# Turning all blocks with 32 by 32 transposes on VectorE and plain DMAs instead of crossbar DMA transposes

## The chip, the core and the metric

The kernel runs on one core of one Trainium2 chip. The metric is the device time of one execution in microseconds (us). A core has TensorE (PE) for matrix products, VectorE (DVE), ScalarE (ACT) and GpSimd (POOL) for elementwise work, and SyncE (SP), which here only issues DMAs. Each engine takes its instructions from a queue of its own, in order. DMAs are issued from the queues of SP and ACT.

## The reference

A layer with two residual parts on x of shape 8 x 2048 x 256 (batch, tokens, width), all in float32:

```
n1 = layernorm(x)
Q = xpos(n1 @ W_Q);  K = xpos_down(n1 @ W_K);  V = n1 @ W_V     # rotary embedding with a scale
p = softmax(Q @ K^T) * 0.9 ** |n - m|                            # softmax over all 2048 keys
x = x + p @ V
n2 = layernorm(x)
h = silu(fp4(n2) @ fp4(w_gate)^T) * (fp4(n2) @ fp4(w_up)^T)      # 704 hidden columns
x = x + fp4(h) @ fp4(w_down)^T
```

`fp4` cuts the last dimension into blocks of 16, divides each by its largest magnitude over 6, rounds to the grid 0, 0.5, 1, 1.5, 2, 3, 4, 6 with sign, and multiplies back.

## The kernel before

Tokens are worked off in 128 blocks of 128 queries, one block to a step: `step(n)` for n = 0 to 127, 16 steps to a batch. Tokens of four blocks form a group of 512; a group is normalized (`statistics`, `normalize`), turned so that the width lies on the partitions (`turn_x`), and projected to q, k (`project_rotated`, `rotate`) and v (`project_v`, `keep_v`). The first four groups are projected before the steps; later ones are prepared inside them, spread over four steps: a group is normalized and turned where n%4 is 0, v is projected where n%4 is 1, k where it is 2 and q where it is 3.

The steps are pipelined by hand: the order of the source is the order in each engine's queue (`manual_schedule`), and step n holds parts of five blocks. It computes the scores of block n against all 2048 keys in two halves (`scores`, L451), their maxima (`maximum`, L463) and exponentials (`exponentials`, L485); turns the exponentials (`turn_p`), so that keys lie on the partitions; multiplies the turned exponentials of block n-1 with the decay (`decays`, L530) and attends (`attend`, L541), where only keys within 7 blocks count, 8 to 15 blocks, because the decay makes the rest vanish; adds the residual and normalizes for the second part (`add_residual`, `normal_scales`); rounds block n-2 to fp4 (class `Fp4`: VectorE with GpSimd, L181 to L222), turns it (`turn_xq`) and multiplies with the gate and up weights (`gate_up`, L605, with the Silu L617 behind it on ScalarE); multiplies, rounds and turns the hidden values of block n-3 (`hidden`, `turn_h`); and brings block n-4 down (`down`, L646; `finish`, L652).

Each turn goes through DRAM: ScalarE splits the 32-bit values into two planes of 16-bit halves (`split`, L231), a DMA from ScalarE's queue stores the planes (`store`, L238), and a transposing DMA from SP's queue brings them back turned (`fetch`, L243). The first four groups and some of the last blocks are turned by TensorE instead, with an identity matrix.

PSUM tiles of the scores, projections, gate and up come from one pool, in turn:

```
ps_s = ctx.enter_context(tc.tile_pool(name="ps_s", bufs=3, space=bass.MemoryType.PSUM))
ps_m = ctx.enter_context(tc.tile_pool(name="ps_m", bufs=2, space=bass.MemoryType.PSUM))
```

A tile waits until the tile that had its buffer before has been read. The weights of the second part are rounded to fp4 and turned once; their stages (`scale_weights`, `round_weights`, `turn_ffn_weights`) are spread over the projection of the first groups and steps 0 to 3 by the table `IN_STEPS`.

Of the kernel before, what the change touches and what calls it, by code (L numbers as in the profile page):

```python
# [9 lines left out]
F32 = mybir.dt.float32  # L10
I32 = mybir.dt.int32
U16 = mybir.dt.uint16
# [10 lines left out]
BAND = 7  # L23
QBLK = 16
# [9 lines left out]
def preln_xpos_retention_fp4_ffn_kernel(  # L34
# [108 lines left out]
    load_tables()  # L143
    load_pair("q", w_q)
    load_tables()
    wv_sb = cpool.tile([P, HC, H], F32, name="wv_sb")
    nc.sync.dma_start(wv_sb, w_v.rearrange("(c p) d -> p c d", p=P))
# [4 lines left out]
    wd_t = cpool.tile([P, FC, H], F32, name="wd_t")  # L152

# [74 lines left out]
    def split(planes, at, src):  # L228

        n = src.shape[-1]  # L230
        nc.scalar.copy(  # L231
            planes[:, :, at : at + n], src.bitcast(U16).rearrange("p (k h) -> p h k", h=2)
        )

    def store(planes, name):
        rows, _, n = planes.shape
        there = dram.tile([rows, 2, n], U16, tag=f"turn{rows}_{n}", name=f"there_{name}")
        nc.scalar.dma_start(there, planes)  # L238
        return there

    def fetch(dst, there):

        nc.sync.dma_start_transpose(dst.bitcast(U16), there.rearrange("q h k -> (q h) k"))  # L243
# [5 lines left out]

    def split_hidden(planes, src):  # L250
        split(planes, 0, src[:, : (FC - 1) * P])
        split(planes, (FC - 1) * P, src[:, F - P :])
# [9 lines left out]
    def load_ffn_weights():  # L262
        for name, src in (("g", w_gate), ("u", w_up)):
            raw = act_p.tile([P, FULL - 1, H], F32, tag="kt", bufs=2 * NG, name=f"w{name}_rows")
            nc.sync.dma_start(
                raw, src[: (FULL - 1) * P, :].rearrange("(c p) k -> p c k", p=P)
            )
            weight_rows[name] = raw
        whole = act_p.tile([P, 2 * GROUP], F32, tag="kt", bufs=2 * NG, name="wgu_rows")
        raw = whole[:, : 3 * H].rearrange("p (c k) -> p c k", c=3)  # L270
        for c, src in enumerate((w_gate, w_up)):
            nc.sync.dma_start(raw[:, c, :], src[(FULL - 1) * P : FULL * P, :])
            nc.sync.dma_start(raw[c * REST : (c + 1) * REST, 2, :], src[FULL * P :, :])
        weight_rows["r"] = raw
        scratch["r"] = whole[:, 3 * H :]
        big = act_p.tile([P, 2 * GROUP], F32, tag="kt", bufs=2 * NG, name="wbig")
        down_rows = []
        for c in range(HC):
            down_rows.append(act_p.tile([P, BPG * H], F32, tag="vt", bufs=6, name=f"wd_rows{c}"))
            weight_rows["d", c] = down_rows[c][:, :F]  # L280
            scratch["gu"[c]] = down_rows[c][:, F:]
        for key in "gur":
            raw = weight_rows[key].rearrange("p c k -> p (c k)")
            weight_fp4[key] = Fp4(raw, P, raw.shape[-1], f"w{key}", big, scratch[key])
        for c in range(HC):
            weight_fp4["d", c] = Fp4(weight_rows["d", c], P, F, f"wd{c}")

    def load_decay_and_down():
        nc.sync.dma_start(decay_sb, decay)
        for c in range(HC):  # L290
            nc.sync.dma_start(weight_rows["d", c], w_down[ts(c, P), :])

    def turn_ffn_weights(key):
        raw = weight_rows.pop(key)
        planes = prob_p.tile([P, 2, 2 * GROUP], U16, tag="planes", bufs=3, name=f"pl_w{key[0]}")
        if key[0] == "d":
            planes = planes[:, :, : FC * P]
            split(planes, 0, raw[:, : (FC - 1) * P])
            nc.vector.memset(planes[:, :, (FC - 1) * P : (FC - 1) * P + LAST].bitcast(F32), 0.0)
            split(planes, (FC - 1) * P + LAST, raw[:, (FC - 1) * P :])  # L300
            fetch(wd_t[:, :, ts(key[1], P)], store(planes, f"wd{key[1]}"))
        elif key == "r":
            planes = planes[:, :, : 3 * H]
            split(planes, 0, raw.rearrange("p c k -> p (c k)"))
            there = store(planes, "wr")
            for c, dst in enumerate((wg_t, wu_t)):
                fetch(dst[:, :, (FULL - 1) * P : FULL * P], there[:, :, c * H : (c + 1) * H])
                fetch(dst[:, :, FULL * P :], there[c * REST : (c + 1) * REST, :, 2 * H :])
        else:
            n = FULL - 1  # L310
            for kc in range(HC):
                nc.scalar.copy(
                    planes[:, :, kc * n * P : (kc + 1) * n * P].rearrange("p h (c k) -> p h c k", c=n),
                    raw.bitcast(U16)[:, :, kc * 2 * P : (kc + 1) * 2 * P].rearrange(
                        "p c (k h) -> p h c k", h=2
                    ),
                )
            there = store(planes, f"w{key}")
            dst = {"g": wg_t, "u": wu_t}[key]
            for kc in range(HC):  # L320
                fetch(
                    dst[:, kc, : n * P].rearrange("p (c r) -> p c r", c=n),
                    there[:, :, kc * n * P : (kc + 1) * n * P],
                )
# [6 lines left out]
    def round_weights(key):  # L331
# [4 lines left out]
        (0, "exponentials"): [(round_weights, "u")],  # L336
        (0, "end"): [(round_weights, "r"), (turn_ffn_weights, "u")],
        (1, "decays"): [(scale_weights, ("d", 1))],
        (1, "end"): [(turn_ffn_weights, "r")],
        (2, "decays"): [(round_weights, ("d", 0))],  # L340
        (3, "exponentials"): [(turn_ffn_weights, ("d", 0))],
        (3, "decays"): [(round_weights, ("d", 1))],
        (3, "end"): [(turn_ffn_weights, ("d", 1))],
    }

    def weights_in_step(n, place):
        for stage, key in IN_STEPS.get((n, place), ()):
            stage(key)
# [20 lines left out]

    def turn_x(k):  # L370
        xt = groups.pop(k)
        xn_t = act_p.tile([P, BPG, HC, P], F32, tag="xn_t", bufs=3, name=f"xnt_{k}")
        if k < NG:
            pt = ps_s.tile([P, BPG, HC, P], F32, tag="s", name=f"pt_x_{k}")
# [3 lines left out]
            for c in range(0, BPG, 2):  # L378
                nc.scalar.copy(xn_t[:, c : c + 2], pt[:, c : c + 2])
        else:  # L380
            planes = prob_p.tile([P, 2, 2 * GROUP], U16, tag="planes", bufs=3, name=f"pl_x{k}")
            split(planes, 0, xt.rearrange("p c d -> p (c d)"))
            fetch(xn_t.rearrange("p c h t -> p (c h) t"), store(planes, f"x{k}"))
# [21 lines left out]
    def rotate(k, name):  # L405
# [12 lines left out]
        load_tables()  # L418
# [21 lines left out]
    total = B * NB  # L440

# [34 lines left out]
    stored, turned = {}, {}  # L476

    def exponentials(n):

        nmax = raw_scores.pop(n)  # L480
        sums = small.tile([P, 2], F32, tag="sums", name=f"sums_{n}")
        prs = []
        for half in range(2):
# [8 lines left out]
            prs.append(pr)  # L492
        stored[n] = []
        for half in range(2):
            keys = keys_of(n, half)
            if keys and n == total - 1:
                stored[n] = (keys, prs[half][:, (keys[0] - half * HALF) * P :])
            elif keys:
                w, at = len(keys) * P, (keys[0] - half * HALF) * P
                planes = prob_p.tile([P, 2, HALF * P], U16, tag="planes", bufs=3, name=f"pl_{n}_{half}")  # L500
                split(planes, 0, prs[half][:, at : at + w])
                stored[n].append((keys, store(planes[:, :, :w], f"p{n}_{half}")))
        prob[n] = sums

    def turn_p(n):
        p_t = prob_p.tile([P, 2 * BAND + 1, P], F32, tag="p_t", name=f"p_t_{n}")
        if n == total - 1:
            keys, pr = stored.pop(n)
            pt = ps_s.tile([P, HALF, P], F32, tag="s", name=f"pt_p_{n}")
            for j in range(len(keys)):  # L510
                nc.tensor.transpose(pt[:, j, :], pr[:, ts(j, P)], ident)
            turned[n] = (p_t, pt)
            return
        first = stored[n][0][0][0]
        for keys, there in stored.pop(n):
            fetch(p_t[:, keys[0] - first : keys[-1] + 1 - first, :], there)
        turned[n] = (p_t, p_t)
# [7 lines left out]
    def decays(n):  # L525
        keys, (p_t, pt) = band(n), turned[n]
        for c in range(0, len(keys), BPG):
            w = min(BPG, len(keys) - c)
            d0 = keys[c] - n % NB + BAND
            nc.vector.tensor_tensor(  # L530
                p_t[:, c : c + w, :], pt[:, c : c + w, :], decay_sb[:, d0 : d0 + w, :], ALU.mult
            )

    attended = {}

    def attend(n):
        b, i = divmod(n, NB)
        po = ps_m.tile([P, H], F32, tag="m", name=f"o_{n}")
        keys, (p_t, _) = band(n), turned.pop(n)
# [10 lines left out]
    def inverse_sum(n):  # L550
        sums = prob[n]
        rs = small.tile([P, 1], F32, tag="rs", name=f"rs_{n}")
        nc.vector.tensor_tensor(rs, sums[:, 0:1], sums[:, 1:2], ALU.add)
        nc.vector.reciprocal(rs, rs)
        prob[n] = rs
# [3 lines left out]
    def add_residual(n):  # L559
        x1 = ffn_p.tile([P, H], F32, tag="x1", bufs=5, name=f"x1_{n}")  # L560
# [21 lines left out]
    def turn_xq(n):  # L582
        x1, xq, _ = mid.pop(n)
        xq_t = ffn_p.tile([P, HC, P], F32, tag="xq_t", bufs=1, name=f"xq_t_{n}")
        if n >= total - 2:
# [3 lines left out]
            nc.scalar.copy(xq_t, pt)  # L589
        else:  # L590
            planes = ffn_p.tile([P, 2, FC * P], U16, tag="hplanes", name=f"pl_xq{n}")[:, :, :H]
            split(planes, 0, xq)
            fetch(xq_t, store(planes, f"xq{n}"))
# [263 lines left out]
```

## Time and profile before

| | |
|---|---|
| median of 3 runs | 2896.73 us (2894.92 to 2897.74) |
| the profiled execution | 2900.07 us, its span 2898.2 us |
| busy PE, DVE, ACT, POOL | 2826.7, 2280.1, 1431.8, 1410.7 us |
| mean granted TensorE clock | 0.990 |
| DMA | 446.24 MB in 892828 packets, 730992 of them under 512 B |
| SP's queue (q1), ACT's queue (q10) | 43.0% and 18.4% of 16 engines' span |

The profile is of one execution. A row of its groups gives line, engine, operation, what is written from what, the count, then busy time and mean duration, then the idle time of the engine just before and what ended it. A line of the waits names who waited for whom, in total, how often, and the longest. A timeline row gives start, duration, engine and instruction. A row of the DMA issues gives the size of each and the median time from issue to landing. PE's busy time is modelled from pipelined matrix products, so a few us of it are uncertain.

### The profile page before, as it was taken

The page shows a single profiled execution, that of the slowest core. Times are in us where ns is not written, and L with a number is a line of the kernel's source. Part 1 is how long each engine was busy: PE and PEld are TensorE (multiplying, and loading weights), DVE is VectorE, ACT ScalarE, POOL GpSimd, SP SyncE. Part 2 cuts the span into 40 slices and gives each one's busy share as a digit, 9 for nine tenths or more (in the row PEclk, how much of TensorE's full clock was granted, in tenths as well). Part 3 has the DMA queues.
Part 4 walks back from the last instruction along what each step waited for, and adds up shares of the span by engine and source line. Part 5 has one row for each costly group of instructions (what it writes and reads, how often), then busy time and mean ns, then how long its engine had stood idle before and what let it go on. Part 6 is the DMA issues. An engine that isn't in the chain of part 4 may idle for free.

```text
span 2898.2 us, 31875 instructions
## 1 busy us (share of the span) xinstructions
PE 2826.7 (98%) x9668; PEld 1839.3 (63%) x9668; DVE 2280.1 (79%) x5249; ACT 1431.8 (49%) x1592; POOL 1410.7 (49%) x1328
## 2 busy tenths in 40 slices
PE   7789999999999999999999999999999999999997
PEld 4456666666666666666666666666666666666665
DVE  7677788777888777877877878877788877777787
ACT  2345455554555554555554555554454554455552
POOL 5455454544554445544455454454445454444443
PEclk9899999999999999999999999999999999999998
DMA  5567565775567665577565666566656666546651
GB/s 177 143 152 176 147 162 140 179 177 142 144 166 160 169 165 142 152 180 172 147 159 145 162 170 161 144 175 160 167 144 157 160 171 145 141 125 147 159 133 43
DMA packets 892828, 446.24 MB, mean 154 GB/s; under 512 B 730992, under 2 KB 839920, under 8 KB 892656
## 3 DMA queue, kind: packets, MB, share of 16 engines
q1 hardware_dynamic: 786640, 266.04, 43.0%
q10 hardware_dynamic: 106016, 178.16, 18.4%
q8 instruction: 77, 1.26, 0.2%
q14 instruction: 95, 0.78, 0.1%
HBM read 71.04 MB, written 194.90 MB: 92 GB/s over the span
## 4 chain that ended last, share of the span: by engine, by line
PE 81%; DVE 9%; POOL 4%; issue 2%; DMA 2%; ACT 1%; ACTq 0%; SPq 0%; POOLq 0%; DVEq 0%
PE s L451 26%; PE o L541 18%; PE d L646 10%; PE gate L605 9%; PE up L605 9%; PE pp_k L394 3%; PE pp_q L394 3%; PE pv L425 3%; DVE m L463 1%; DVE p_t L530 1%; POOL h L221 1%; POOL h L220 1%; DMA xq_t<-there_xq 1%; POOL h L222 1%; DVE h L215 1%
## 5 line engine op out<-in xcount | busy, mean ns | idle before, releaser
L451 PE MATMUL s<-kt,qt 128*128 128x512 f32 x2048 | 909.0, 596 | 13.7 <-ACT h L617 7.8
L451 PEld LDWEIGHTS s<-kt,qt 128*128 128x128 f32 x2048 | 389.4, 191 | 478.0 <-issue 419.6
L541 PE MATMUL o<-v,p_t 128*128 128x256 f32 x2944 | 658.6, 380 | 8.2 <-DVE p_t L530 8.2
L541 PEld LDWEIGHTS o<-v,p_t 128*128 128x128 f32 x2944 | 560.4, 191 | 87.4 <-DVE p_t L530 9.9
L220 POOL TENSOR_TENSOR h<-h,big_h 128x704 f32<-128x704 f32 x126 | 212.1, 1684 | 553.2 <-DVE big_h L219 549.1
L463 DVE TENSOR_REDUCE m<-s 128x1 f32<-128x1024 f32 x256 | 310.3, 1213 | 97.8 <-PE s L451 97.2
L231 ACT COPY pl<-p 128x2048 uint16<-128x2048 uint16 (+7 forms) x239 | 357.6, 1496 | 58.1 <-ACT pl L231 49.5
L646 PE MATMUL d<-wd_t,h_t 128*128 128x256 f32 x1536 | 360.8, 385 | 14.5 <-issue 4.4
L231 ACT COPY pl_xq<-xq 128x512 uint16<-128x512 uint16 x126 | 77.8, 618 | 600.7 <-POOL xq L222 600.7
L646 PEld LDWEIGHTS d<-wd_t,h_t 128*128 128x128 f32 x1536 | 294.8, 193 | 102.2 <-issue 38.6
L485 ACT ACT_TABLE_LOAD x125 | 160.4, 1283 | 352.1 <-DVE nmax L468 301.3
L605 PE MATMUL gate<-wg_t,xq_t 128*128 128x352 f32 x1024 | 324.4, 460 | 4.4 <-DMA xq_t<-there_xq 3.9
L605 PE MATMUL up<-wu_t,xq_t 128*128 128x352 f32 x1024 | 323.8, 459 | 0.0
L231 ACT COPY pl_h<-h 128x1280 uint16<-128x1280 uint16 x248 | 194.0, 829 | 250.3 <-POOL h L222 248.3
L485 ACT ACTIVATE p<-s,nmax 128x1024 f32<-128x1024 f32 x256 | 282.8, 1110 | 20.0 <-DVE nmax L468 17.8
L195 POOL TENSOR_TENSOR h<-h,inv_h 128x704 f32<-128x704 f32 x126 | 174.5, 1385 | 225.8 <-DVE inv_h L193 225.8
L605 PEld LDWEIGHTS up<-wu_t,xq_t 128*128 128x128 f32 x1024 | 194.6, 190 | 108.3
L605 PEld LDWEIGHTS gate<-wg_t,xq_t 128*128 128x128 f32 x1024 | 194.0, 190 | 94.3 <-ACT pl L231 4.2
L530 DVE TENSOR_TENSOR p_t<-p_t,decay_sb 128x512 f32<-128x512 f32 (+3 forms) x414 | 243.7, 645 | 1.3 <-DMA p_t<-there_p 1.3
L195 POOL TENSOR_TENSOR xq<-xq,inv_x 128x256 f32<-128x256 f32 x127 | 78.8, 620 | 302.1 <-DVE inv_x L193 299.7
L221 POOL TENSOR_TENSOR h<-h,big_h 128x704 f32<-128x704 f32 x126 | 211.6, 1679 | 9.9
L220 POOL TENSOR_TENSOR xq<-xq,big_x 128x256 f32<-128x256 f32 x127 | 92.3, 726 | 238.7 <-DVE big_x L219 238.7
(139 smaller groups left out, 3475.9 us busy)
## 6 DMA issues: line engine op xcount, KB each, us to landing
there_p<-pl ACTq DMA_DIRECT2D x127, 512.0 KB, 3.2
there_h<-pl_h ACTq DMA_DIRECT2D x124, 384.0 KB, 4.1
rope_k<-in_rope_dram SPq DMA_DIRECT2D x32, 512.0 KB, 4.5
rope_q<-in_rope_dram SPq DMA_DIRECT2D x32, 512.0 KB, 4.9
xr<-in_L_attn_X_dram SPq DMA_DIRECT2D x128, 128.0 KB, 3.2
out_dram<-x SPq DMA_DIRECT2D x128, 128.0 KB, 3.5
there_xq<-pl_xq ACTq DMA_DIRECT2D x126, 128.0 KB, 2.1
x<-in_L_attn_X_dram SPq DMA_DIRECT2D x31, 512.0 KB, 4.8
```

The source lines that it names most:

```text
L195: self.wide_on.tensor_tensor(self.v3, self.v3, self.wide(inv), ALU.mult)
L220: self.wide_on.tensor_tensor(v, v, big, ALU.add)
L221: self.wide_on.tensor_tensor(v, v, big, ALU.subtract)
L231: nc.scalar.copy(planes[:, :, at : at + n], src.bitcast(U16).rearrange("p (k h) -> p h k", h=2))
L394: nc.tensor.matmul(pp[:, half, :], w_pair[name][:, hc, half, :], xn_t[:, :, hc, :], start=(hc == 0), stop=(hc == HC - 1),)
L451: nc.tensor.matmul(ps[:, j, :], q[:, dc, ts(i % BPG, P)], kt[b, half * 2 + j][:, dc, :], start=(dc == 0), stop=(dc == 1),)
L463: nc.vector.tensor_reduce(raw_scores[n][:, half : half + 1], raw_scores[n, half], AX.XY, ALU.max)
L485: nc.scalar.activation(pr, raw_scores.pop((n, half)).rearrange("p j k -> p (j k)"), AF.Exp, bias=nmax, accum_out=sums[:, half : half + 1],)
L530: nc.vector.tensor_tensor(p_t[:, c : c + w, :], pt[:, c : c + w, :], decay_sb[:, d0 : d0 + w, :], ALU.mult)
L541: nc.tensor.matmul(po, p_t[:, j, :], vt[b, k // BPG][:, k % BPG, :], start=(j == 0), stop=(j == len(keys) - 1),)
L605: nc.tensor.matmul(ps[:, half, :FH], xq_t[:, hc, :], w[:, hc, ts(half, FH)], start=(hc == 0), stop=(hc == HC - 1),)
L646: nc.tensor.matmul(pd, h_t[:, fc, :], wd_t[:, fc, :], start=(fc == 0), stop=(fc == FC - 1))
```

## The change

Nine things change; the arithmetic of the result stays what it was.

1. Turns of p, xq, h and x inside the steps no longer use 16-bit planes and transposing DMAs. The new `turn` transposes every 32 by 32 square on VectorE into a tile `sq`, with the squares' columns grouped by quarter; one DMA from ScalarE's queue stores it; four plain DMAs from SP's queue, one for each 32 partitions, bring back rows whose runs are a quarter of the width: 64 elements for xq, 192 for h, 256 for x, 256 to 480 for p. What arrives still has its runs in the order quarter, square, element (`in_runs`).
2. ScalarE copies xq, h and x out of that order (`keep_xq`, `keep_h`, `keep_x`); for p the product with the decay reads through it. `p_t` and the new `runs` have one buffer. `sq` of p and of x is one tile with one buffer; xq and h have their own.
3. Groups after the first are normalized by ScalarE (`normalize_on_scalar`: a negated mean, four passes that add it, four that scale), not by VectorE.
4. The two halves' sums are added by ScalarE behind the exponentials; VectorE keeps the reciprocal.
5. The weights are turned by TensorE with ScalarE copies; their loads, scales, rounds and turns stand at other places.
6. In a step `turn_h` stands after the residual, `turn_x` after `turn_h` and before `normal_scales`; `turn_xq` after the scales of h; step 2 attends before it projects.
7. Tables of the rotation (`load_tables`) are loaded after the attention of a step, not inside `rotate`.
8. Blocks 120 to 123 (`deferred`) keep their turned hidden values in tiles of the keys' pool, and their `down` and `finish` move behind the last step.
9. The memset of `wd_t`'s unused rows moves to the start.

```diff
+    def turn(dst, pieces, name, tag):
+        n = sum(src.shape[-1] for src in pieces) // NSQ
+        sq = prob_p.tile([P, dst.shape[-1]], F32, tag=tag, bufs=1, name=f"sq_{name}")
+        sq = sq[:, : NSQ * n].rearrange("p (c f) -> p c f", c=NSQ)
+        at = 0
+        for src in pieces:
+            w = src.shape[-1] // NSQ
+            nc.vector.transpose(
+                sq[:, :, at : at + w].rearrange("p c (k i) -> p k c i", i=SQ),
+                src.rearrange("p (k c i) -> p k c i", c=NSQ, i=SQ),
+            )
+            at += w
+        there = dram.tile([NSQ, SQ, NSQ, n], F32, tag=f"turn_{n}", name=f"there_{name}")
+        nc.scalar.dma_start(there.rearrange("a i c f -> (a i) c f"), sq)
+        dst = dst[:, : NSQ * n].rearrange("p (a f) -> p a f", a=NSQ)
+        for c in range(NSQ):
+            nc.sync.dma_start(dst[ts(c, SQ)], there[:, :, c, :].rearrange("a i f -> i a f"))
...
+    def normalize_on_scalar(k, blocks=range(BPG)):
+        xt, (mv, rstd) = groups[k], normed.pop((k, blocks))
+        minus = small.tile([P, BPG], F32, tag="minus", bufs=2, name=f"minus_{k}")
+        nc.scalar.mul(minus, mv[:, :, 0], -1.0)
+        for c in blocks:
+            nc.scalar.activation(xt[:, c, :], xt[:, c, :], AF.Identity, bias=minus[:, c : c + 1])
+        for c in blocks:
+            nc.scalar.mul(xt[:, c, :], xt[:, c, :], rstd[:, c : c + 1])
...
-            planes = prob_p.tile([P, 2, 2 * GROUP], U16, tag="planes", bufs=3, name=f"pl_x{k}")
-            split(planes, 0, xt.rearrange("p c d -> p (c d)"))
-            fetch(xn_t.rearrange("p c h t -> p (c h) t"), store(planes, f"x{k}"))
+            xt = groups[k].rearrange("p c d -> p (c d)")
+            turn(xt, [xt], f"x{k}", "sq")
...
+        rs = small.tile([P, 1], F32, tag="rs", name=f"rs_{n}")
+        nc.scalar.activation(rs, sums[:, 0:1], AF.Identity, bias=sums[:, 1:2])
...
+            runs = prob_p.tile([P, (2 * BAND + 1) * P], F32, tag="runs", bufs=1, name=f"runs_{n}")
+            turn(runs, pieces, f"p{n}", "sq")
...
-            planes = ffn_p.tile([P, 2, FC * P], U16, tag="hplanes", name=f"pl_xq{n}")[:, :, :H]
-            split(planes, 0, xq)
-            fetch(xq_t, store(planes, f"xq{n}"))
+            turn(xq, [xq], f"xq{n}", "sq_x")
...
+            turn(h, [h[:, : (FC - 1) * P], h[:, F - P : F]], f"h{n}", "sq_h")
...
     IN_STEPS = {
-        (0, "exponentials"): [(round_weights, "u")],
-        (0, "end"): [(round_weights, "r"), (turn_ffn_weights, "u")],
-        (1, "decays"): [(scale_weights, ("d", 1))],
-        (1, "end"): [(turn_ffn_weights, "r")],
+        (0, "maximum"): [(scale_weights, ("d", 0))],
+        (0, "exponentials"): [(scale_weights, ("d", 1))],
+        (0, "rotation"): [(round_weights, "u")],
+        (0, "attend"): [(turn_ffn_weights, "g")],
+        (1, "decays"): [(round_weights, "r")],
+        (1, "attend"): [(turn_ffn_weights, "u")],
         (2, "decays"): [(round_weights, ("d", 0))],
-        (3, "exponentials"): [(turn_ffn_weights, ("d", 0))],
+        (2, "attend"): [(turn_ffn_weights, "r")],
         (3, "decays"): [(round_weights, ("d", 1))],
+        (3, "attend"): [(turn_ffn_weights, ("d", 0))],
         (3, "end"): [(turn_ffn_weights, ("d", 1))],
     }
...
         scores(n, 1)
+        if on(3):
+            hid[n - 3][2].normalize()
         if on(2):
             turn_xq(n - 2)
-        if on(3):
-            hid[n - 3][2].normalize()
         maximum(n, 1)
+        if on(4) and n - 4 < total - 4:
+            keep_h(n - 4)
         exponentials(n)
+        if on(2) and n - 2 < total - 2:
+            keep_xq(n - 2)
+        for g in kept:
+            keep_x(g)
...
-            normalize(k)
+            normalize_on_scalar(k)
...
-        if on(3) and n < total - 1:
-            turn_h(n - 3)
...
         if on(1):
             add_residual(n - 1)
+        if on(3) and n < total - 1:
+            turn_h(n - 3)
+        if turn_group:
+            turn_x(k)
+            kept.append(k)
+        if on(1):
             normal_scales(n - 1)
         if on(2):
             gate_up(n - 2)
-        if turn:
-            turn_x(k)
         weights_in_step(n, "end")
```

## The prediction

> **What bounds the kernel now.** I read the page's busy line, then busy time by stage, the waits, the timeline of one step, and last the rows that price the new work.
>
> ```profile
> PE 2826.7 (98%) x9668; PEld 1839.3 (63%) x9668; DVE 2280.1 (79%) x5249; ACT 1431.8 (49%) x1592; POOL 1410.7 (49%) x1328
> ```
> ```profile
> 0.00:160.00 160.00, 122.56 (x336) 66.99 (x337) 111.61 (x243) 47.63 (x59) 83.92 (x69) 0.89 0.57 157
> 160.00:2780.00 2620.00, 2601.72 (x8967) 1702.45 (x8966) 2077.67 (x4810) 1342.84 (x1483) 1283.94 (x1219) 1.00 0.63 157
> 2780.00:2898.00 118.00, 102.43 (x368) 69.83 (x366) 90.84 (x197) 41.32 (x51) 42.85 (x40) 0.93 0.30 74
> ```
> Columns of a stage: length, then busy PE, PEld, DVE, ACT, POOL, then clock. In 2620 us of steady steps PE stands still for 18 us. The head loses 37 us and runs at a clock of 0.89, the tail loses 16 us. The steady part has little to give and much to lose.
>
> ```profile
> DVE xq L573 <- POOL rstd_f L159: 155.8, 127, 3.6
> DVE x L561 <- PE o L541: 134.4, 75, 2.9
> PE s L451 <- ACT h L617: 7.8, 7, 3.0
> ```
> VectorE's idle time lies in waits of its own queue, which new work may fill. The third line is the tightest place of the loop: `ps_s` has three PSUM buffers, so the second half of a step's scores takes the buffer that the Silu of the step before has read. The timeline of a step n with n%4=0 and the start of n+1 shows it:
>
> ```profile
> 1479.38 7.03 PE L451 MATMUL s<-kt,qt 128*128 128x512 f32 x16
> 1485.30 0.43 DVE L193 RECIPROCAL inv_h<-scale_h 128x44 f32<-128x44 f32 x1
> 1486.44 1.23 DVE L463 TENSOR_REDUCE m<-s 128x1 f32<-128x1024 f32 x1 [0.72 <-PE s L451]
> 1491.33 0.20 ACT L485 ACTIVATION_READ_ACCUMULATOR p<-s,nmax 128x1 f32 x1
> 1494.17 1.68 POOL L221 TENSOR_TENSOR h<-h,big_h 128x704 f32<-128x704 f32 x1
> 1494.41 0.48 DVE L561 SCALAR_TENSOR_TENSOR x<-o,rs,xr 128x256 f32<-128x256 f32 x1
> 1497.02 3.60 PE L451 MATMUL s<-kt,qt 128*128 128x512 f32 x8
> 1498.95 0.34 ACTq L238 DMA_DIRECT2D there_h<-pl_h  x1
> 1500.61 0.76 ACT L617 ACTIVATE h<-gate 128x704 f32<-128x704 f32 x1
> ```
> From 1479.38 on: exponentials end at 12.15; the scores of n+1 start at 17.64, and their second half is due 3.43 later, at 21.07. The Silu ends at 21.99, which is 2.42 after the store of h was issued (table load and Silu lie between), and PE lost 0.8 us there. This was a step with 8 blocks of attention; each further block gives PE 0.43 us more.
>
> **The change, part by part.**
>
> ```profile
> L181 DVE TENSOR_REDUCE amax_h<-h 128x44 f32<-128x704 f32 x128 | 112.5, 879 | 0.1
> L181 DVE TENSOR_REDUCE amax_x<-xq 128x16 f32<-128x256 f32 x128 | 53.7, 420 | 4.4
> L553 DVE TENSOR_TENSOR rs<-sums 128x1 f32<-128x1 f32 x128 | 153.2, 1197 | 0.0
> L366 DVE TENSOR_SCALAR x<-x,mv,rstd_a 128x256 f32<-128x256 f32 x128 | 44.1, 407 | 4.9 <-POOL rstd_a L159 4.9
> L138 ACT COPY wk_pair<-wk_raw 128x256 f32<-128x256 f32 x2 | 0.7, 416 | 4.0 <-DMA wk_raw<-in_L_attn_W_K_dram 4.0
> ```
> ```profile
> there_p<-pl ACTq DMA_DIRECT2D x127, 512.0 KB, 3.2
> there_xq<-pl_xq ACTq DMA_DIRECT2D x126, 128.0 KB, 2.1
> x<-in_L_attn_X_dram SPq DMA_DIRECT2D x4, 128.0 KB, 2.4
> ```
> *VectorE.* No row is a 32x32 transpose. The two reductions give 156 ns + 1.025 ns per element[...]. L219 (538 ns for 704, 294 for 256) would be the floor, 155 + 0.545 per element; twice the reduction the ceiling. I take the reductions, as a transpose also reads one f32 stream: p (11.5 blocks, 1472 elements, 1.9 instructions) 1.81 us, xq 0.42, h (640+128) 1.10, x (1024) 1.21. Over 127, 126, 124 and 28 uses: 230 + 53 + 136 + 34 = 453 us. L553 goes: it is a one-column addition of two SBUF operands, and its 1197 ns last until the GpSimd instruction beside it ends, so 153 us go and nothing is put behind it but a reciprocal (164 ns). Would a transpose be held in the same way? L561 above, with one SBUF tensor, takes its usual 0.48 us in the middle of L221; a transpose has one, so I say no. L366 goes for 31 groups (1.38 us each): -43. Sum 2280 + 453 - 153 - 43 = 2537 us, 87%; floor 2370, ceiling 2990. Most of it falls into the waits above: the transposes of h stand where VectorE waited for rstd_f, those of p where L553 stood, those of xq in the 0.72 us before L463.
>
> *ScalarE.* All splits go (358 + 78 + 194 us by their groups); copies of h (0.8 us), xq (0.4), x (1.0), a one-column sum (about 0.25) and the normalization come. Less work, but in one queue, in order. The Trainium skill says that additions and multiplications belong on VectorE, not ScalarE ("ScalarE: Activation LUTs", Rules for kernel authors), which speaks against this part. Rows: four L366 take 1.38 us; ScalarE needs eight passes at 0.37 to 0.45 (L138) plus the negated mean, about 4.3 us with the waits on its own results. By load alone the rule costs nothing (ScalarE is at 49%); by place it decides, as follows.
>
> *Where it lands.* In a step with n%4=0 ScalarE's order is: exponentials, sum, copy of xq, eight normalizing passes, then the store of p, store of h, store of x, Silu. The copy of xq waits for the new round trip: transposed at 6.3 to 6.75 (in VectorE's gap), store issued 6.85, 2.2 us to SP's start as now, four loads at 0.5 each, the last landing 2.2 after its issue: 12.8, copied by 13.2. Passes to 17.4. The store of p, issued there, lands at 20.6. And the tile `sq`, one buffer, serves p and x: the transposes of x (`turn_x`) wait for that landing. They end at 21.75, the store of x is issued at 21.85, the Silu ends 2.42 later at 24.3, instead of 21.07 due. PE waits 3.2 us, now 0.8. For 11, 15 and 12 blocks PE is due at 22.4, 24.1, 22.8; p's store has 768, 960, 704 KB, at the page's 0.0027 us per KB more (512 against 64 KB, 3.2 against 2.0) the Silu ends at 25.0, 25.5, 24.8: waits 2.6, 1.4, 2.0. Four such steps cost 2.4 + 2.6 + 1.4 + 2.0 = 8.4 us more than now; 27 steps turn a group in the loop after n=1: **+56 us**. Bounds: were p to land by 17.4, nothing; with each term at its slow end (passes 0.5, loads 3 us) 1.5 us more per step, +96.
>
> Queued on VectorE behind the stalled transposes, by their durations in the same timeline: normal scales to 24.2, L623 (it needs the Silu, 24.3) 25.2, rounding xq 26.2, largest h 27.1, first maximum 28.2, scales of h 30.3, xq turned 30.7, second maximum 32.1, first decay product 32.8. PE, itself late, ends the scores at 27.9 and after v (3.46) and `down` (2.59) wants the product at 34.0: no second stall. In the steps with n%4=1, along statistics, `turn_p`, residual, `turn_h`, the Silu ends within 0.2 us of PE's need, so up to 1 us each (+27) goes in the range. `gate` waits 0.4 us for xq in 7 steps: +3.
>
> *DMA.* A turn is now one store and four plain loads of 32 partitions: SP issues some 15 DMAs a step for 7 before, 8 us of 22.6 at 0.5 each; `load_tables`, moved behind p's loads, still has most of a step before its rotation, and `runs` and `p_t` with one buffer are overwritten only after the product and the attention of the step before, over 10 us earlier: nothing for these; if SP were late by a step, the rotation would wait some 4.5 us. The skill warns that a plain DMA that transposes by strides is 19 times slower than the crossbar one ("VectorE: DVE Perf Modes", The three transpose paths). By that rule xq's 2.7 us would become 51 and every step stop. But it speaks of large innermost strides; here the elements are already turned and runs are 256 to 1920 bytes. The row near it is the x load, 1 KB runs, 2.4 us. I use the row, and leave the rule a rival.
>
> *Weights.* 34 transposes on PE at 0.11 us (L377, eight in 0.87): +4. Their scale and round stages are moved on DVE and POOL, the loads behind x and tables on SP, `wd_t`'s memset to POOL's start. The head's waits before (6.8 us at L394, 7.4 at L541, 3.6 and 2.4 for POOL's rotation of kt) change: without L366 of groups 2 and 3, VectorE reaches the second rotation 7 us sooner, and the first scores end near 53 instead of 62.7; but at n=1 eight passes, p's store and the weights' copy stand before `keep_v`, for which the scores of step 2 wait some 10 us. I take -10, range -25 to +10.
>
> *Tail.* Four `down` (2.59 us each) leave the last four steps, which then are VectorE's (some 17.7 for 19.5): -7; at the end they fill PE's gaps, keep its clock up (L646 5.5 for 2.75 now), and add four L652 (0.41): -1.
>
> **Sum:** 56 + 3 + 4 - 10 - 8 = +45 on the profiled execution's 2900.1 us, 2945; that execution is 3.3 above the median, so 2942.
>
> **The rivals.** *(A) The shared `sq` buffer*, above: 2942, chance 0.57. For it: the order in ScalarE's queue and the 0.8 us that PE loses there already. *(B) All is hidden, faster:* if p's store lands by about 17.4 (passes overlapping, loads quick), the Silu ends before 21 to 24, PE runs through and even the 8 us of waits for it now go: 4 - 10 - 8 - 8 = -22, 2875. It decides where p's landing comes 3 us earlier than I have it. 0.17. *(C) VectorE becomes the bound:* transposes at half rate, 3.6 us more a step, 23.4 busy for PE's 22.0, and up to 1 us a step that it can't fill: 2995 to 3120; held by GpSimd like L553, only p's: about 2975. 0.18. *(D) Plain loads slow* at 256 bytes: xq 2.5 us later, n%4=0 and 1 wait for it, 64 x 1 to 2.5 on top of A: 3000 to 3100. 0.08.
>
> **How the numbers follow.** A's own range is 2905 to 2985. 0.2% (6 us) is what a measurement here tells from no change. Faster: B, but for 0.02, and 0.01 of A: 0.16; same: 0.02 of B, 0.04 of A: 0.06; slower the rest, 0.78. The range 2878 to 3025 leaves out the better half of B (0.08) and the upper parts of C and D (0.12).
>
> **What would show it.** Right: PE's scores waiting for Silu some 1.5 to 3 us at n%4=1, about 27 times; the x transposes waiting for p's store; PE's busy time near 2820; DVE at 85 to 88%; a transposed 1024 at 1.2 us; ScalarE busy near 1150. Wrong: no such wait (B), a transpose over 2 us for 1024 elements or held while GpSimd runs (C), `gate` waiting for the copy of xq in most steps (D).

## The result, and the profile after

The changed kernel takes 2936.84 us (median of 4 runs, 2931.39 to 2941.99) against 2897.23 us of the kernel before in the same session: a ratio of 1.0138, 95% interval 1.0118 to 1.0157, slower by 39.6 us. Its profiled execution took 2931.39 us, span 2929.6; before, 2900.07 and 2898.2. The two profiles thus differ by 31.4 us, and these are what can be located. The profiled execution of the changed kernel is its fastest, with a mean granted clock of 0.994; the other three have 0.991 or 0.992 and take 5 to 11 us more (see the last section).

First the busy line and the stages of the changed kernel, with the same columns as before (length; busy PE, PEld, DVE, ACT, POOL; clock, DMA share, GB/s):

```profile
PE 2827.4 (97%) x9702; PEld 1840.6 (63%) x9702; DVE 2469.3 (84%) x5636; ACT 1075.9 (37%) x1637; POOL 1412.5 (48%) x1329
```
```profile
0.00:160.00 160.00, 130.89 (x403) 76.17 (x404) 118.08 (x257) 52.77 (x103) 88.34 (x75) 0.94 0.44 139
160.00:2780.00 2620.00, 2565.70 (x8831) 1676.58 (x8830) 2233.24 (x5109) 980.27 (x1475) 1267.83 (x1201) 1.00 0.52 155
2780.00:2929.00 149.00, 130.85 (x472) 87.89 (x470) 118.02 (x272) 42.82 (x60) 56.37 (x54) 0.98 0.29 92
```

PE's work is as long as before, 2827 us. In the same 2620 us of the middle PE now stands still for 54 us, not 18. The waits (total, times, longest) name what it stands for:

```profile
PE d L677 <- ACT h_t L668: 57.9, 41, 3.0
...
PE o L561 <- DVE p_t L546: 16.5, 6, 5.6
...
PE s L473 <- ACT h L641: 3.8, 2, 3.4
...
DVE sq_x L237 <- DMA there_p<-sq_p: 3.2, 5, 1.4
```

The first line is new and larger than the whole loss: `down` (L677) waits for `h_t`, the copy of the turned hidden values. The last two are those that the prediction built on. The scores' wait for the Silu shrank (7.8 before, 3.8 now), and the x transposes wait 3.2 us for p's store in the whole kernel.

Where it lies is seen from PE's first score matmul in each step. For steps 16 to 111, six batches, the mean length by place in the batch is:

| n mod 16 | 0 | 4 | 8 | 12 | 1 | 5 | 9 | 13 | the other eight |
|---|---|---|---|---|---|---|---|---|---|
| before, us | 17.65 | 18.94 | 20.67 | 19.37 | 23.05 | 23.07 | 24.18 | 22.61 | |
| after, us | 19.00 | 20.83 | 23.38 | 21.22 | 21.10 | 22.82 | 24.12 | 22.39 | equal within 0.01 |

The steps with n%4=0, where no projection stands between the scores and `down`, lose 7.80 us a batch; those with n%4=1 win 2.48; six times the difference is the +32.0 of this stretch. The steps 112 to 126, which have no projections, lose 10.4: from 114 to 123 PE stands at least 1.06 us in each. The head wins: step 0 starts 2.9 us earlier, steps 0 to 15 are 5.9 shorter in all (step 7 starts 14.4 earlier, then steps 8 and 12 lose 5.6). The last step's start to the end is 2.2 shorter. Sum: 32.0 + 10.4 - 2.9 - 5.9 - 2.2 = +31.4.

Two timelines of the changed kernel show the wait (start, duration, engine, instruction, in brackets the idle time before and its releaser). The first is a step that begins at 1485.49:

```profile
1482.24 1.04 DVE L237 STREAM_TRANSPOSE sq_h<-h 128x640 f32<-128x640 f32 x2
...
1483.31 0.33 ACTq L243 DMA_DIRECT2D there_h<-sq_h  x1
...
1485.49 7.03 PE L473 MATMUL s<-kt,qt 128*128 128x512 f32 x16
...
1486.72 1.74 SPq L246 DMA_DIRECT2D h<-there_h  x4
...
1491.79 0.39 DVE L237 STREAM_TRANSPOSE sq_xq<-xq 128x256 f32<-128x256 f32 x1
...
1492.21 0.33 ACTq L243 DMA_DIRECT2D there_xq<-sq_xq  x1
...
1492.73 0.83 ACT L668 COPY h_t<-h 128x768 f32<-128x768 f32 x1 [7.01 <-DVE sq_xq L237]
...
1493.62 2.86 PE L677 MATMUL d<-wd_t,h_t 128*128 128x256 f32 x12 [1.09 <-ACT h_t L668]
```

The scores end at 1492.52 and `down` is next on PE, but on ScalarE the copy L668 stands behind the issue of xq's store, which waits for VectorE's transposes of xq. In another such step, begun at 1304.26, it is the landing of h itself:

```profile
1303.96 0.43 SPq L106 DMA_DIRECT2D rope_q<-in_rope_dram  x1
...
1304.44 0.57 SPq L684 DMA_DIRECT2D out_dram<-x  x1
...
1306.42 2.43 SPq L246 DMA_DIRECT2D h<-there_h  x4
...
1313.14 0.83 ACT L668 COPY h_t<-h 128x768 f32<-128x768 f32 x1 [8.61 <-DMA h<-there_h]
...
1314.03 2.86 PE L677 MATMUL d<-wd_t,h_t 128*128 128x256 f32 x12 [2.74 <-ACT h_t L668]
```

SP issued the rotation table of the next group (512 KB) and the output ahead of h's loads. That happens where n%4 is 2 and 3, and a block turned where n%4=3 is brought down where n%4=0.

### The profile page after: what moved, and what is told of

Read it like the earlier page. It is cut to its first block, busy times and chain, and to the rows that moved or that the text cites. A ratio compares the mean times of both kernels' runs of the same rounds, so it can differ in the third digit from the quotient of the medians.

```text
span 2929.6 us, 34597 instructions
## 1 busy us (share of the span) xinstructions
PE 2827.4 (97%) x9702; PEld 1840.6 (63%) x9702; DVE 2469.3 (84%) x5636; ACT 1075.9 (37%) x1637; POOL 1412.5 (48%) x1329
## 3 DMA queue, kind: packets, MB, share of 16 engines
q8 instruction: 76, 1.25, 0.2%
## 5 line engine op out<-in xcount | busy, mean ns | idle before, releaser
L561 PE MATMUL o<-v,p_t 128*128 128x256 f32 x2944 | 663.7, 382 | 16.5 <-DVE p_t L546 16.5
L668 ACT COPY h_t<-h 128x768 f32<-128x768 f32 x120 | 99.8, 832 | 855.7 <-DMA h<-there_h 422.1
L677 PE MATMUL d<-wd_t,h_t 128*128 128x256 f32 x1488 | 348.6, 384 | 57.9 <-ACT h_t L668 57.9
L677 PEld LDWEIGHTS d<-wd_t,h_t 128*128 128x128 f32 x1488 | 280.9, 191 | 150.6 <-ACT h_t L668 91.7
L546 DVE TENSOR_TENSOR p_t<-runs,decay_sb 128x512 f32<-128x512 f32 (+3 forms) x414 | 235.0, 625 | 7.2 <-DMA runs<-there_p 3.7
L237 DVE STREAM_TRANSPOSE sq_p<-p 128x1024 f32<-128x1024 f32 (+7 forms) x239 | 223.3, 969 | 0.0
L581 DVE SCALAR_TENSOR_TENSOR x<-o,rs,xr 128x256 f32<-128x256 f32 x124 | 60.0, 483 | 154.0 <-PE o L561 150.6
```

What stands on the lines that cost most here:

```text
L237: nc.vector.transpose(sq[:, :, at : at + w].rearrange("p c (k i) -> p k c i", i=SQ), src.rearrange("p (k c i) -> p k c i", c=NSQ, i=SQ),)
L546: nc.vector.tensor_tensor(p_t[:, c:to, :].rearrange("p k (a i) -> p k a i", a=NSQ), pt[:, c:to], decay_sb[:, d0 + c : d0 + to, :].rearrang ...
L561: nc.tensor.matmul(po, p_t[:, j, :], vt[b, k // BPG][:, k % BPG, :], start=(j == 0), stop=(j == len(keys) - 1),)
L677: nc.tensor.matmul(pd, h_t[:, fc, :], wd_t[:, fc, :], start=(fc == 0), stop=(fc == FC - 1))
```

## The experiments

Each kernel is the changed one with the edit shown, or with the edits named; times are medians, ratios are to the kernel before in the same session and have their 95% interval. The kernel before took 2897.2 to 2901.1 us in these sessions, so a difference of medians from two sessions can be some 4 us off; where it matters I give what the ratios make of it too. Theory H: h's new round trip, with its copy, ends after `down` is due. Theory A: the prediction's shared buffer. Theory V: VectorE's added work.

**A buffer of its own for x.**
```
-            turn(xt, [xt], f"x{k}", "sq")
+            turn(xt, [xt], f"x{k}", "sq_g")
```


> The x turns get a buffer of their own, so that turn_x no longer waits for the landing of p's store. Theory A of the prediction (the shared buffer holds the Silu and with it the next scores, +56 us): 2937 falls by about 56 to some 2881. Theory H (h's new round trip ends after `down` is due; 53 us of PE's waits before L677 in the steps with n%4=0 and in the last 16): the trace of the changed kernel has only 0.2 to 0.3 us of wait at the x transposes, so 0 to -3 us, 2934 to 2937. Theory C (VectorE's load is the bound): no change.

Measured: 2944.80 us, ratio 1.0159 (1.0137 to 1.0181); the changed kernel has 1.0138. Nothing of the 56 us comes back, though the wait of the x transposes for p's store, 3.2 us in the changed kernel, is gone from the trace. Theory A falls for this kernel.

**The copy of h ahead of xq's store.**
```
+        if on(4) and n - 4 < total - 4:
+            keep_h(n - 4)
         if on(2):
             turn_xq(n - 2)
         maximum(n, 1)
-        if on(4) and n - 4 < total - 4:
-            keep_h(n - 4)
```


> keep_h stands before turn_xq, so on ScalarE the copy of h is no longer queued behind the store of xq, which waits for VectorE's transposes of xq. Theory H: 21 of PE's waits before L677 (22 us) had a copy that was released by the transposes of xq; these go, the 17 whose copy was released by the landing of h (32 us) stay: -15 to -22, 2915 to 2922. Theory A and theory C: no change, or up to +5 as xq lands later.

Measured: 2939.98, ratio 1.0149 (1.0131 to 1.0166): no gain, a miss for H as I had it. In the trace no copy is released by xq's transposes any more, but 32 of the 34 waits before `down` now follow a late landing of h, and PE waits nearly as long (53.9 us). The steps with n%16=0 and 12 became shorter by 0.8 and 0.25 us, those with 4 and 8 longer by 1.3 and 1.1. In these two the landing of h came last already, so there was nothing to win; and with the copy first, xq's store waits for h's landing (in n%16=8 it leaves 9.0 us into the step, not 6.7).

**The turn of h ahead of the residual.**
```
+        if on(3) and n < total - 1:
+            turn_h(n - 3)
         if on(1):
             add_residual(n - 1)
-        if on(3) and n < total - 1:
-            turn_h(n - 3)
```


> turn_h stands before add_residual again, as in the kernel before, so h's store leaves about 1.3 us earlier. Theory H: only the 17 waits that ended with the landing of h shrink, and not below the 1.06 us that the queue behind xq sets: 32 - 17 x 1.06 = 14 us at most, so -8 to -14, 2923 to 2929. Theory A: the Silu's chain is not moved by this, no change. Theory C: no change.

Measured: 2958.55, ratio 1.0210 (1.0196 to 1.0224): slower. One line of its waits shows what the edit did to VectorE (13.4 us in 14 places in the changed kernel):

```profile
DVE sq_h L237 <- POOL h L221: 166.1, 99, 3.8
```

VectorE now stands in front of the transposes of h until GpSimd has rounded h, and the residual stands behind them. PE's wait for h_t grew to 65.8 us, not less, and that for decay products from 16.5 to 20.0.

**`down` behind the attention on PE.**
```
-        if on(4) and n - 4 not in deferred:
-            down(n - 4)
         ...
         if on(1) and n != 2:
             attend(n - 1)
+        if on(4) and n - 4 not in deferred:
+            down(n - 4)
```


> On PE `down` of block n-4 follows the attention of block n-1 instead of standing before it: it is due about 3.5 to 6.5 us later, nothing else is moved. Theory H: the whole wait before L677 goes (53 us), and at most some 5 to 10 us of waits of the attention for the decay products come: -40 to -53, 2884 to 2897. Theory A and theory C: no change (2937).

Measured: 2995.67, ratio 1.0336 (1.0322 to 1.0350): far slower, and no test of H. I moved `down` on PE but left `finish` where it was on VectorE, ahead of the residual:

```profile
DVE x L683 <- PE d L677: 262.8, 103, 5.5
...
PE o L561 <- DVE p_t L546: 101.2, 44, 5.4
```

PE's wait for h_t is gone but for 1.9 us; VectorE blocks on `down` instead, and the attention, due earlier on PE, waits for decay products.

**The table loads behind h's loads.**
```
-        for name, g in parts(n):
-            if name != "v":
-                load_tables()
         if on(4) and n - 4 not in deferred:
             finish(n - 4)
         ...
             turn_h(n - 3)
+        for name, g in parts(n):
+            if name != "v":
+                load_tables()
```


> The load of the next rotation table (512 KB, in the steps with n%4 = 2 and 3) is issued by SP behind h's four loads instead of ahead of them and of the output. Theory Q (h's loads are late because in SP's queue, and on the DMA engines, the 512 KB table goes ahead of them in the very steps before n%4=0): the 17 waits before L677 that ended with the landing of h shrink to the 1.06 us that the copy behind xq's store sets, -10 to -20, 2917 to 2927. Theory S (h's trip is simply too long in its serial parts: transposes behind the residual, store 3.6, four issues 1.7, landing 2 to 3, copy 0.8): no change, within 5 us of 2937.

Measured: 2916.18, ratio 1.0052 (1.0039 to 1.0064): 20.7 us of the 39.6 come back by the medians, 25 by the ratios, 15.5 between the two profiled executions. The five executions now agree within 1.4 us, at a mean clock of 0.995. The longest wait of `down` falls from 3.0 to 1.5 us:

```profile
PE d L677 <- ACT h_t L668: 45.1, 41, 1.5
```

What the table had delayed is the transfer, not the issue: over the steps with n%4=3 from 19 to 107, the first of h's loads follows its store by 4.05 us in the changed kernel and 4.01 here, but the latest copy of h begins 7.61 us into the next step instead of 9.13.

**Both: table loads late and the copy of h first.** The edit is the sum of the second and the fifth.

> The same, and the copy of h stands before the transposes of xq as in e2_keep_h_first. Theory Q: both causes of the wait before L677 are gone in the steps with n%4=0, -30 to -45, 2892 to 2907. Theory S: as e2_keep_h_first, 2935 to 2942.

Measured: 2899.33, ratio 0.9995 (0.9986 to 1.0003): 37.5 us come back (41 by the ratios), and the kernel is level with the one before. Both edits are needed: the copy alone brought nothing, together with the table it brings 17 us beyond the table.

```profile
PE d L677 <- ACT h_t L668: 26.1, 27, 2.1
```

**The copy in two halves,** on top of that:
```
-        nc.scalar.copy(
-            h_t.rearrange("p c (a i) -> p c a i", a=NSQ), in_runs(h) if src is None else src
-        )
+        to = h_t.rearrange("p c (a i) -> p c a i", a=NSQ)
+        src = in_runs(h) if src is None else src
+        for c in range(0, FC, FC // 2):
+            nc.scalar.copy(to[:, c : c + FC // 2], src[:, c : c + FC // 2])
```


> As e6_tables_keep, and the copy of h into h_t is two copies of three chunks each, so that `down` can begin about 0.4 us earlier. Theory H (what is left of the wait before L677, 26 us in 27 places, is the end of h's serial trip): 0.4 us less in each, -8 to -15 against e6_tables_keep, 2884 to 2892. Theory V (VectorE's queue sets those steps, and PE would wait for the decay products instead): no change, 2896 to 2903.

Measured: 2887.41, ratio 0.9962 (0.9949 to 0.9976), 11.9 us less (10 by the ratios). 0.4 us on the end of h's trip is worth that much over 27 waits; VectorE, whose work is the same, does not set these steps.

```profile
PE d L678 <- ACT h_t L671: 14.3, 18, 1.6
```

**Only h back to planes and the crossbar.**
```
-            turn(h, [h[:, : (FC - 1) * P], h[:, F - P : F]], f"h{n}", "sq_h")
         ...
+            planes = ffn_p.tile([P, 2, FC * P], U16, tag="hplanes", bufs=1, name=f"pl_h{n}")
+            split(planes, 0, h[:, : (FC - 1) * P])
+            split(planes, (FC - 1) * P, h[:, F - P : F])
+            fetch(h_t, store(planes, f"h{n}"))
         ...
-        if on(4) and n - 4 < total - 4:
-            keep_h(n - 4)
```
`split`, `store` and `fetch` come back from the kernel before.

> Only h goes back to ScalarE's split into planes and one transposing DMA straight into h_t; p, xq and x stay with VectorE's transposes, all else as in the changed kernel. Theory H (h's trip with its copy is what the change loses by): the wait before L677 (53 us) goes, and with it the slower matmuls behind each wait; steps with n%4=0 return to about 17.7, 19.0, 20.7 and 19.4 us as before, the steps with n%4=1 keep what they won: -50 to -70, 2867 to 2887, faster than the kernel before. Theory V (VectorE's 189 us more, and not h, is what the change loses by): VectorE is relieved of h's 136 us of transposes in the middle of each step, so -10 to -30 at most and waits of the attention for the decay products stay: 2907 to 2927.

Measured: 2897.82, ratio 0.9987 (0.9978 to 0.9995): 39 us come back (44 by the ratios), less than H's 50 to 70 and more than V's 30. With the table still ahead, `down` keeps a part of its wait:

```profile
PE d L702 <- DMA h_t<-there_h: 14.6, 17, 2.4
```

**The same with the table loads late.** The edit is the sum of this one and the fifth.

> As e7_h_planes (h by planes and a transposing DMA, the rest new), and the table loads behind h's load in SP's queue. Theory Q: the 17 waits of `down` for the landing of h that e7_h_planes still had (14.6 us, and the slower matmuls behind them) shrink, -10 to -20, 2878 to 2888. Theory V: the wait passes to the attention, which waits for decay products: 2893 to 2900.

Measured: 2881.84, ratio 0.9945 (0.9933 to 0.9958). The cost of the table ahead of h is now shown twice: 21 us by the medians and 25 by the ratios with the new way of turning h, 16 and 12 with the old. The steps 16 to 111 take 2094.9 us, 6.5 fewer than in the kernel before.

**The group normalized by VectorE again.**
```
-            normalize_on_scalar(k)
+            normalize(k)
```


> A group is normalized by VectorE's four L366 again (1.4 us a group) instead of ScalarE's eight passes and the negated mean (4.3 us); nothing else. By the prediction's theory A the passes hold p's store and through it the Silu: -56, about 2881. By the Trainium skill's rule (additions and multiplications on VectorE) a gain as well. Theory H: the passes are off the path; VectorE's 1.4 us come before p's transposes, which wait for the exponentials there: 2932 to 2942, no change.

Measured: 2958.27, ratio 1.0192 (1.0179 to 1.0206): slower than the changed kernel by 0.0054 of the ratio (16 us; 21 by the medians), where one theory expected a large gain and the other none. PE's wait for h_t hardly grew (57.9 before the edit), while its busy time rose from 2827.4 to 2846.4 us:

```profile
PE d L677 <- ACT h_t L668: 61.2, 46, 3.0
```

Of these 19 us, 10 lie in the steps with n%4=0 of 16 to 111, where PE ran at a lower clock behind a wait in seven steps, in the profiled execution of the changed kernel in one (last section). Besides, the head is 6.5 us longer than in the changed kernel and the steps with n%16=1 lose 1.0 us each.

**Without the deferral of four `down`,** on top of planes and late tables:
```
-    deferred = {n: None for n in range(total - 8, total - 4)}
+    deferred = {}
     ...
-    first, second, third, fourth = deferred
-    down(first)
     ...
```
The other `down` and `finish` of the deferred blocks behind the last step go too.

> As e10_planes_tables, without the deferral of four `down` to the end. The prediction's step (-7 in the last four steps, -1 at the end): 8 us slower than e10_planes_tables. What the trace of the changed kernel suggests (in steps 124 to 126 PE stands 2.2 to 3.0 us for decay products, so the deferred 2.6 us were only turned into waiting, and come once more at the end into PE's gaps): within 4 us of e10_planes_tables.

Measured: 2879.61, ratio 0.9936 (0.9924 to 0.9948) against 0.9945: the same. In steps 124 to 126 PE stands 2.2 to 2.3 us each with the deferral and 0.4 to 0.9 without; at the end it stands 9.6 and 15.2.

**And the buffer of its own for x,** on top of that, as in the first experiment.

> As e11_no_deferral, and the transposes of x have a buffer of their own. In e11_no_deferral VectorE does wait there for the landing of p's store (60.1 us in 28 places, up to 4.7), the very wait that the prediction's theory A priced at 56 us of the kernel's time. Theory A: 2880 falls by about 50, to some 2830. Theory H: the Silu behind it still ends before PE wants its buffer (8.2 us of such waits in the whole trace), so the wait is slack of VectorE: 2872 to 2882, within 0.3% of e11_no_deferral.

Measured: 2875.73, ratio 0.9913 (0.9899 to 0.9927), the fastest of all, 0.87% faster than the kernel before. In the kernel without this edit the predicted wait of VectorE does exist:

```profile
DVE sq_x L238 <- DMA there_p<-sq_p: 60.1, 28, 4.7
```

It goes entirely; in its place VectorE waits less, for ScalarE's passes over x:

```profile
DVE sq_x L238 <- ACT x L395: 14.2, 12, 2.0
```

The kernel gains 3.9 us by the medians, 0.0023 +- 0.0018 by the ratios (1 to 12 us). So even there A's wait is nearly all slack of VectorE.

## Why the prediction was right and where it was wrong

The direction was right and the sum close (+45 of the profiled execution predicted, +31.3 found), but the largest term stood for a mechanism that is not there, and the true one was missed. That the sum came near is luck: +56 stood for a wait of 3 us, and the 37 to 41 us of h's trip stood at nothing.

*The shared buffer `sq`, +56: measured 3.2 us of wait, and no gain without it.* The step that failed is "Passes to 17.4. The store of p, issued there, lands at 20.6." The same stretch after the change, in a step begun at 1485.49:

```profile
1500.42 0.49 ACT L379 ACTIVATE x<-x,rstd_a 128x256 f32<-128x256 f32 x1
...
1500.61 0.33 ACTq L243 DMA_DIRECT2D there_p<-sq_p  x1
...
1500.82 1.29 ACT L379 ACTIVATE x<-x,rstd_a 128x256 f32<-128x256 f32 x3
...
1502.31 1.04 DVE L237 STREAM_TRANSPOSE sq_h<-h 128x640 f32<-128x640 f32 x2 [0.99 <-POOL h L221]
...
1503.51 1.25 DVE L237 STREAM_TRANSPOSE sq_x<-x 128x1024 f32<-128x1024 f32 x1 [0.17 <-DMA there_p<-sq_p]
...
1506.47 0.76 ACT L641 ACTIVATE h<-gate 128x704 f32<-128x704 f32 x1
```

The passes run at a pitch of 0.43 us and end at 16.6; the store is issued at 15.1, while they still run, and has landed by 18.0. VectorE would not have reached x sooner anyhow: it waited for GpSimd's rounding of h until 1502.31. The Silu ends at 21.7 instead of 24.3. The change even took away waits: steps with n%4=1 became shorter by 15 us in 16 to 111, 12 of them in the one behind n%16=0. There PE had waited 0.8 us for the Silu and on average 0.65 for xq in each of the six batches, and both are gone; of the waits for xq these are the lines of before and after:

```profile
PE gate L605 <- DMA xq_t<-there_xq: 3.9, 6, 1.6
```
```profile
PE gate L629 <- ACT xq_t L615: 0.5, 1, 0.5
```

For the Silu that was rival B's mechanism, whose point of decision, p landed by about 17.4, was nearly reached.

*The DMAs costed at nothing.* "`load_tables`, moved behind p's loads, still has most of a step before its rotation" is true of the table. The step names who waits for the table, but not what is queued behind it: h's loads. That costs 20.7 us (fifth experiment; 25 by the ratios). The other part, the copy of h queued behind xq's store on ScalarE and 0.83 us long, is not in the text at all; I priced the "copies of h (0.8 us)" as ScalarE's load and never set the end of h's trip against the time when `down` is due, 7.0 us into a step with n%4=0. The two parts are worth 37.5 us together (41 by the ratios).

*VectorE.* The transposes are what the reductions said:

```profile
L237 DVE STREAM_TRANSPOSE sq_p<-p 128x1024 f32<-128x1024 f32 x127 | 154.9, 1220 | 0.0
...
L237 DVE STREAM_TRANSPOSE sq_h<-h 128x640 f32<-128x640 f32 x124 | 104.8, 845 | 13.7 <-POOL h L221 13.4 <-issue 0.3
...
L237 DVE STREAM_TRANSPOSE sq_xq<-xq 128x256 f32<-128x256 f32 x126 | 48.9, 388 | 1.3 <-POOL xq L221 1.3
...
L237 DVE STREAM_TRANSPOSE sq_x<-x 128x1024 f32<-128x1024 f32 x28 | 33.9, 1211 | 3.2 <-DMA there_p<-sq_p 3.2
```

The durations of all sizes together are 452.6 us for the predicted 453, and the longest of 1024 elements takes 1.25 us, so none was held by GpSimd. The page's busy time is 2469 against my 2537 mainly because it counts a time once in which two instructions overlap: the two transposes of an h have 845 and 269 ns but take 1.04 us together (at 1502.31 above), and with the overlaps taken out the transposes add some 404 us, not 453. That is about 48 of the 68 us; the rest I did not trace. Rival C stays out: the half copies run as fast as 2887 us with VectorE at 86%.

*ScalarE and the rule.* Busy 1076 for about 1150. The Trainium skill's rule ("ScalarE: Activation LUTs", Rules for kernel authors: additions and multiplications on VectorE) would have cost 16 to 21 us here. The prediction was right that load does not decide; it was wrong on which side the place decides, since the passes delayed nothing in the timeline above.

*Loads.* Rival D fell: four loads of 32 KB for xq land 1.8 us after issue at runs of 256 bytes, and `gate` waits 0.5 us in all for xq.

*Head -10, tail -8, weights +4.* The head won 14.4 by step 7 and 8.9 by step 16. The last four steps did not shorten: 124 to 126 took 58.9 us before and 59.4 after, because "which then are VectorE's" holds, but at no less than before: the attention moves up and waits for decay products (16.5 us in 6 places in the whole kernel, 7.9 of them in these three steps). The end gained 2.2. The eleventh kernel confirms that the deferral as a whole gives nothing. The weights were not measured apart.

## What to carry to other kernels

When a transfer is moved in a queue, list what stands behind it as well as who waits for it, and follow each of those to its consumer in the step where that consumer is due earliest; here a projection of some 3.5 us gives most steps a slack that every fourth one lacks. A round trip through memory has an end on each engine that it touches: set the sum of transposes, store, issues, landing and copy against the due time, and look for what is queued ahead of the last link. Two causes of one wait hide each other, so an edit that removes one may show nothing until both are gone.

## What the runs showed of the hardware that I had not expected

A standstill of PE costs more than its length. In the 240 steps with n%4=0 between 16 and 111 of ten of these kernels (before, after, and the experiments but for the half copies, the planes with late tables and the last two), a step without a gap in PE's work has the busy time of the kernel before. Of 133 steps whose longest gap was 0.05 to 1.95 us, 131 have at most 0.3 us more, mostly 0.27. (The ends of matrix products are modelled, so this 0.27 may belong to the gap.) Of 42 with 1.95 to 2.4 us, 24 have 1.5 us more or over, mostly 1.95; of 16 with 2.4 to 3.0 us 8, and of 6 with 3.0 us or more all. Wherever a gap of 1.95 us or more cost that much, the granted clock over the next 4 us was 0.50 to 0.66; where it did not, 1.00. In the second experiment, around a gap of 4.45 us (a row of the timeline, then stretches with the columns as above):

```profile
2300.15 4.54 PE L677 MATMUL d<-wd_t,h_t 128*128 128x256 f32 x12 [4.45 <-ACT h_t L668]
```
```profile
2285.00:2295.00 10.00, 10.00 (x28) 5.15 (x28) 8.26 (x23) 2.04 (x2) 5.81 (x8) 1.00 0.70 210
2295.00:2300.00 5.00, 0.70 (x2) 0.00 (x0) 4.84 (x11) 0.74 (x1) 1.38 (x1) 1.00 0.67 180
2300.00:2304.00 4.00, 3.85 (x10) 3.07 (x11) 2.67 (x5) 3.94 (x7) 2.40 (x2) 0.57 0.24 66
2304.00:2308.00 4.00, 4.00 (x21) 3.51 (x20) 0.98 (x3) 3.75 (x11) 2.34 (x2) 1.00 0.19 76
```

The granted clock is 0.57 in the 4 us after the gap, then full, and `down` takes 4.54 us instead of 2.86. The Trainium skill ("TensorE: Matmul & The Clock Gate", Why this matters for your kernels) asks for no idle gaps of more than about 3 us; here all 6 gaps of 3.0 us or more cost, and 32 of the 58 between 1.95 and 3.0 us too. Which of these cost looks like chance: in the profiled execution of the changed kernel none of 6 did (one of 1.90 us did), in that of the kernel with VectorE's normalization 7 of 9. It is a likely reason, not a shown one, why the changed kernel's other executions take 5 to 11 us more, three to six such costs of 1.7 us by my estimate from 1.95 less 0.27: only the fastest has a trace. With the tables late, where these steps had no gap over 1.5 us, the executions agree within 1.4 us. The changed kernel itself pays 0.27 us in 23 of its 24 steps with n%4=0 in 16 to 111, and 1.95 in one, together 8.1 us beside the waits.

A DMA in ScalarE's queue was issued while passes that stand ahead of it still ran: at 1500.61, with passes until 1502.11, in the timeline above. Of the 2.6 us by which p landed earlier than theory A had it (18.0 for 20.6), 1.5 are this.
